# One image earlier through the steps: the norm, the statistics, a ScalarE copy and the ranking of a two-layer codebook convolution are moved

## The chip, the core and the metric

The kernel runs on one core of a Trainium2 chip. Its engines are TensorE (PE; its weight loads are listed as PEld), VectorE (DVE), ScalarE (ACT), GpSimd (POOL) and SyncE (SP, which here only issues DMAs). The metric is the device time of one execution in microseconds (us). Three runs of the kernel before gave 2716.25, 2726.48 and 2731.89 us; the median is 2726.48 us.

## What is computed

The input holds 16 images of 256 channels and 28 x 28 positions. Each image is normalised in groups of 8 channels (`_gn`), goes through two codebook convolutions with a batch norm each, through a squeeze-and-excitation gate, and is added to its input twice.

```python
def amm_conv3x3(x, centroids, w_sub, stride=1):
    p = patches(x, 3x3).reshape(B, C, 9, Ho * Wo).transpose(0, 3, 1, 2)
    d = sum(p * p) - 2.0 * einsum('bncs,cks->bnck', p, centroids) + sum(centroids * centroids)
    attn = softmax(-d)                                   # over 16 centroids of each channel
    lut = einsum('cks,cso->cko', centroids, w_sub)
    return einsum('bnck,cko->bno', attn, lut)
...
out = amm_conv3x3(x, centroids1, wsub1)
out = relu(bn_inference(out, ...))
out = amm_conv3x3(out, centroids2, wsub2)
out = se_layer(bn_inference(out, ...), se_w1, se_b1, se_w2, se_b2)
return relu(out + x)
...
x = x + _L0_conv_ref(_gn(x), ...)
```

## The kernel before, in words

All 16 images pass through layer 1, then all 16 through layer 2. An image of a layer is cut into four blocks: two halves of the channels (`hh`) times two halves of the rows (`t`). `BLOCKS` gives the order. Every block takes two steps, so an image takes eight; image n of the 32 (16 in each layer) starts at step g = 8n. "Step 0 to 7" below means the step within its image.

The order is written out by hand. `at(step, sub, function, ...)` puts a job into a table; the jobs are sorted by step and by `sub` and issued in that order. Every engine and every DMA queue takes its instructions strictly in the order of issue, so the place of a job decides behind what it waits.

Block j (g = 2j) goes this way:

- `patches` (L366, L370) loads the shifted rows of the image from its home in DRAM (`home1` in layer 1, `home2` in layer 2) into one of two patch buffers `pt`. It is issued two steps ahead, at `sub` 1.5, six DMAs on SyncE's queue for each half block.
- `logits` (L382) are 32 small matmuls on TensorE for a group of 32 channels (one of four: `mm`), two groups in each of two steps, at `sub` 0.1 and 1.1. `exps` (L393) on ScalarE follows each. In the first half of layer 2's channels, group 0 goes the `wide_` way through VectorE and GpSimd, so that the largest logit is subtracted.
- Two steps after its start, `num_b` (L446) makes the denominators and the last numerator; `split_r` (ScalarE), `join_r` and `recip_dve` (VectorE) turn them into reciprocals, and `spread` (L485, L489, VectorE shuffles) copies these to the rows of the numerators.
- Three steps after its start, `num_a` (L432) makes the other numerators in four rounds, in the order `SLOT_MM`. Each round writes its own pair of PSUM banks. A round is either multiplied by its spread reciprocal on VectorE (`scale_a`, L508) or copied on ScalarE (`copy_a`, L502) and multiplied on GpSimd (`scale_q`, L497). The rounds that ScalarE copies are called `kept`: before, the last round, and the last two where the next block is a wide one.
- `mix` (L523, L525, GpSimd) makes differences of numerators; `product` (L516, TensorE) multiplies numerators by the look-up tables, 63 k-slices an image in seven combinations. Seven steps of an image have nearly a full product; the product of step 7 has a single slice.

Because four pairs of PSUM banks rotate (`ROLES`), the second pair of the odd step's second logits takes the bank pair of numerator round 1, and the odd step's product that of round 2.

In layer 1 the next image is prepared beside this: `load_x` (L158) loads it to `xt`, `gn_stats` (L314, L315, VectorE), `gn_mean` and `gn_var` (TensorE, VectorE, and GpSimd at L254 to L341) make the statistics, `gn_apply` (L347, ScalarE) writes the normalised image into `xpads`, and `to_home1` (L359, SyncE) stores it twice to `home1`. The first patches of the next image are read from there; they are issued at step 6, `sub` 1.5. Layer 1's outputs are summed in `hpads`, normalised by `norm_out` (L567, ScalarE), and scattered by `to_home2` (L588, indirect DMAs on GpSimd's queue), one scatter waiting for the one before to land. In layer 2, `norm_both` (L580), `se_hidden`, `se_gate`, `se_recip` and the `finish_` jobs make the gate and the sums.

Image 0 of layer 1 gives the channels' ranking for layer 2: `rank_make`, `rank_sum`, `rank_look` and `rank_cols` make row numbers, and `h0_load` and `h0_put` put image 0's rows into `home2`.

Of the kernel before, what the change touches and what calls it, by code (L numbers as in the profile page):

```python
# [8 lines left out]
F32 = mybir.dt.float32  # L9
# [8 lines left out]
P = 128  # L18
# [20 lines left out]
KO = (2, 3, 4, 5, 6, 7, 8, 0, 1)  # L39
SLOT_MM = (1, 2, 3, 0)  # L40
BLOCKS = ((0, 0), (0, 1), (1, 1), (1, 0))
# [32 lines left out]
def kernel(  # L74
# [20 lines left out]
    nc = tc.nc  # L95
# [150 lines left out]
    nc.gpsimd.tensor_scalar(gmat, gmat, 1.0 / 8.0, None, op0=ALU.mult)  # L246
    mhalf = const.tile([P, NB], F32, name="mhalf")
    nc.gpsimd.memset(mhalf, -0.5)
    nc.vector.memset(xpads[0], 0.0)
# [560 lines left out]
    def se_gate(b, step=None):  # L810
        ps = small_bank("sep", step)[:, :NB]
        nc.tensor.matmul(ps, lhsT=w2_sb, rhs=se[b], start=True, stop=True)  # L812
        gt = small.tile([P, NB], F32, name="se_gt")
        for k in range(NB):
            nc.scalar.activation(  # L815
                gt[:, k : k + 1], ps[:, k : k + 1], AF.Exp, bias=nb2_sb[:, k : k + 1], scale=-1.0
            )
        se[b] = gt

    def se_recip(b):  # L820
        nc.vector.tensor_scalar_add(se[b], se[b], 1.0)  # L821
        nc.vector.reciprocal(se[b], se[b])  # L822
# [89 lines left out]
    for j, u in enumerate(blocks):  # L912
# [3 lines left out]
        for p in range(2):  # L916
            u["pt", p] = pts[p]
            at(g + p - NPT, 1.5, patches, u, p, nc.gpsimd if 0 < g + p < 5 else None)
            for q in range(2):
                mm = 2 * p + q  # L920
                at(g + p, 0.1 + q, logits, u, mm)
                if wide and mm == 0:
                    at(g, 0.12, wide_copy, u, mm)
                    at(g, 0.9, wide_turn, u, mm)
                    at(g, 1.38, wide_max, u, mm)
                    at(g, 1.39, wide_sub, u, mm)
                    at(g + 1, 1.22, wide_back, u, mm)
                    at(g + 1, 1.95, wide_exp, u, mm)
                else:
                    at(g + p, 0.12 + q, exps, u, mm)  # L930
        kept = SLOT_MM[2 if wide_next(j) else 3 :]
        at(g + 2, 1.0, num_b, u)
# [5 lines left out]
        for i, mm in enumerate(SLOT_MM):  # L938
# [3 lines left out]
            else:  # L942
                at(g + 2, 2.05 if i == 1 + (len(kept) == 1) else 1.4 + 0.01 * i, spread, u, mm)
                at(g + 3, 1.04 + 0.001 * i, scale_a, u, mm)
# [4 lines left out]
    for l in range(2):  # L949
        for b in range(B):  # L950
# [23 lines left out]
            if l == 0 or b == B - 1:  # L974
                at(g + 11, 1.9, norm_out, l, b, *c12)
                at(g + 11, 1.91, norm_out, l, b, *c22)
                at(g + 12, 1.9, norm_out, l, b, *c11)
                at(g + 13, 0.3, norm_out, l, b, *c21)
            else:
                for o in range(NB):  # L980
                    at(g + 12 + o, 0.3 if o else 1.9, norm_both, b, o)
            if l == 0:
# [8 lines left out]
                if b + 1 < B:  # L991
                    at(*((g - 2, 2.6) if b else (2, 1.65)), load_x, b + 1)
                    for q in range(NB):
                        at(*((g + q, 1.9) if b else (3, 1.9)), gn_stats, b + 1, q)
                    at(g + 3 - 2 * (b > 0), 2.1, gn_mean, b + 1, step=g + 3 - 2 * (b > 0))
                    at(g + 4 - (b > 0), 2.1, gn_var, b + 1, step=g + 4 - (b > 0))
                    for q in range(NB):
                        at(g + 5, 1.9, gn_apply, b + 1, q)
                        at(g + 5, 1.92, to_home1, b + 1, q)
            else:  # L1000
                last = b == B - 1
                at(*((g + 11, 0.6) if last else (g + 13, 2.6)), load_x, b, last)
                at(g + 13, 2.1, se_hidden, b, g + 13)
                at(*((g + 14, 1.05, se_gate, b, g + 14) if last else (g + 17, 2.1, se_gate, b, g + 17)))
# [28 lines left out]
    for o in range(2):  # L1033
        at(15, 1.9, rank_make, o)
        at(17, 1.9, rank_sum, o)
        at(17, 1.95, rank_look, o)
    for o in range(2):
        at(18 + o, 2.7, rank_cols, o)
        at(20 + 2 * o, 0.6, h0_load, o)
        for r in range(2):  # L1040
            at(*(((21, 1.77), (21, 1.808)), ((23, 2.7), (25, 1.78)))[o][r], h0_put, o, r)
        at(32 + 2 * o, 0.6, codes_load, o)
# [217 lines left out]
```

## Time and profile before

| What | Value |
|---|---|
| median of three runs | 2726.48 us |
| the profiled execution | 2734.72 us |
| its span in the profile | 2733.2 us |
| VectorE, ScalarE, GpSimd busy | 65%, 49%, 70% of the span |
| mean granted TensorE clock | 0.988 of full speed |
| data moved by DMA | 374.37 MB |

In the profile's rows the first figures are a start and a length in us, or, in a group, the sum of busy time and the mean of one instruction in ns. `L382` is line 382 of the kernel. `out<-in` names the tiles written and read. What stands in brackets is the engine's idle time in front of the instruction and what ended it: `[3.51 <-DMA pt<-home]` says that the engine stood 3.51 us until a DMA from `home` to `pt` had landed. `SPq` rows are DMAs that SyncE issues. A view of waits gives, for an instruction and what released it, the total in us, the number of times and the longest. The window view gives the busy time of each engine in a stretch, then the granted clock, the DMA engines' busy share and GB/s.

### The profile page before, as it was taken

What the parts mean: (1) busy time and instruction counts of PE and PEld (TensorE: products, weight loads), DVE (VectorE), ACT (ScalarE), POOL (GpSimd) and SP (SyncE); (2) the same over time, 40 slices, a digit from 0 to 9 for tenths busy, and PEclk for the clock granted to TensorE, in tenths of its full rate; (3) what the DMA queues carried; (4) which work ended last, traced back from release to release, by engine and by line L of the source; (5) the groups of instructions that cost most, each with busy time, mean ns of one, the idle gap of its engine ahead of it and who ended that gap; (6) DMA issues with size and microseconds to landing.
All of it is one profiled execution on the core that took longest, in us unless ns stands there. A gap on an engine that the chain in (4) does not pass through costs nothing. (4 is left out here: it accounts for less than half of the span.)

```text
span 2733.2 us, 85665 instructions
## 1 busy us (share of the span) xinstructions
PE 2636.8 (96%) x36984; PEld 1274.1 (47%) x36984; DVE 1785.9 (65%) x3802; ACT 1347.5 (49%) x1857; POOL 1902.5 (70%) x1333
## 2 busy tenths in 40 slices
PE   5899999999999999999999999999999999999997
PEld 2444444444444444444444444444444444444443
DVE  4666565566655566556567677677776786767675
ACT  2444444444444444444454555555555555555553
POOL 3755676656666567665577777877787877787786
PEclk9999999999999999999999999999999999999999
DMA  8665667755666666765485554545555545555541
GB/s 187 151 147 146 143 166 192 186 135 129 161 166 155 150 145 166 171 168 147 112 186 135 113 124 110 122 106 117 121 120 119 117 108 112 124 122 119 117 109 53
DMA packets 223335, 374.37 MB, mean 137 GB/s; under 512 B 30360, under 2 KB 193736, under 8 KB 222952
## 3 DMA queue, kind: packets, MB, share of 16 engines
q1 hardware_dynamic: 216008, 334.87, 54.0%
q0 software_dynamic: 6944, 33.95, 3.6%
q8 instruction: 295, 4.83, 0.8%
q14 instruction: 88, 0.72, 0.1%
HBM read 288.93 MB, written 79.80 MB: 135 GB/s over the span
## 5 line engine op out<-in xcount | busy, mean ns | idle before, releaser
L525 POOL TENSOR_TENSOR qp<-qp,qp 128x784 f32<-128x784 f32 x512 | 943.0, 1865 | 191.2 <-DVE qp L508 190.8
L393 ACT ACTIVATE e<-lg 128x784 f32<-128x784 f32 x960 | 739.2, 821 | 674.2 <-PE lg L382 667.2
L516 PE MATMUL acc<-qp,w_S 128*128 128x392 f32 x2048 | 739.5, 501 | 6.5 <-POOL qp L525 3.8
L382 PE MATMUL lg<-pt,wd 32*32 32x392 f32 x16384 | 516.0, 509 | 57.1 <-DMA pt<-home 49.7
L489 DVE STREAM_SHUFFLE rb<-r 128x392 f32<-128x392 f32 x1024 | 550.3, 603 | 0.0
L516 PE MATMUL acc<-qp,w_A 128*128 128x392 f32 x1536 | 546.5, 499 | 0.1
L516 PEld LDWEIGHTS acc<-qp,w_S 128*128 128x128 f32 x2048 | 375.8, 190 | 354.6 <-POOL qp L525 31.3
L460 DVE SCALAR_TENSOR_TENSOR r<-nb,kst,r 128x392 f32<-128x392 f32 x128 | 79.6, 622 | 568.3 <-ACT r L456 558.6
L516 PEld LDWEIGHTS acc<-qp,w_A 128*128 128x128 f32 x1536 | 284.1, 190 | 250.2 <-DVE qp L508 30.0
L446 PE MATMUL nb<-e,cwb 64*32 64x392 f32 x8192 | 389.7, 510 | 0.7 <-ACT e L393 0.7
L432 PE MATMUL na<-e,cwa 64*32 64x392 f32 x8192 | 376.1, 494 | 0.0
L508 DVE TENSOR_TENSOR qp<-na,rb 128x784 f32<-128x784 f32 x352 | 322.0, 967 | 38.0 <-PE na L432 29.4
L474 DVE RECIPROCAL r<-r 128x392 f32<-128x392 f32 x128 | 333.2, 2603 | 4.4
L497 POOL TENSOR_TENSOR qp<-qp,rb 128x784 f32<-128x784 f32 x160 | 296.8, 1865 | 3.2 <-ACT e L393 0.4
L382 PEld LDWEIGHTS lg<-pt,wd 32*32 32x32 f32 x16384 | 131.9, 103 | 347.4 <-issue 235.1
L497 POOL TENSOR_TENSOR qo<-qo,rb 128x392 f32<-128x392 f32 x128 | 131.3, 1026 | 215.2 <-DVE rb L485 215.1
L446 PEld LDWEIGHTS nb<-e,cwb 64*32 64x32 f32 x8192 | 187.4, 110 | 199.7 <-issue 49.2
L432 PEld LDWEIGHTS na<-e,cwa 64*32 64x32 f32 x8192 | 185.1, 106 | 181.9 <-issue 83.9
L502 ACT COPY qp<-na 128x784 f32<-128x784 f32 x160 | 126.9, 814 | 137.7 <-PE na L432 134.6
L456 ACT ACTIVATE r<-nb,kst 128x392 f32<-128x392 f32 x128 | 86.7, 678 | 185.3 <-PE nb L446 183.2
L588 POOL DMA_INDIRECT home<-hpad,col x60 | 60.4, 1007 | 159.2 <-DMA home<-hpad,col 85.8
L417 POOL TENSOR_TENSOR z<-z,mx 128x1568 f32<-128x1568 f32 x32 | 92.0, 2876 | 97.8 <-DVE mx L411 97.8
(153 smaller groups left out, 1768.2 us busy)
## 6 DMA issues: line engine op xcount, KB each, us to landing
pt<-home SPq DMA_DIRECT2D x768, 209.0 KB
pt<-home SPq DMA_DIRECT2D x756, 104.5 KB
home<-xpad SPq DMA_DIRECT2D x31, 899.0 KB
xt<-in_x SPq DMA_DIRECT2D x30, 784.0 KB
out_dram<-y SPq DMA_DIRECT2D x32, 392.0 KB
w_S<-d_wS SPq DMA_DIRECT2D x4, 576.0 KB
st<-in_wsub SPq DMA_DIRECT2D x4, 512.0 KB
st<-d_wa SPq DMA_DIRECT2D x16, 128.0 KB
```

Of the source, the lines that this page charges most:

```text
L382: nc.tensor.matmul(bk[32 * c : 32 * c + 32, :N].rearrange("p (r w) -> p r w", w=W), lhsT=wts["wd", u["hh"]][32 * i : 32 * i + 32, mm, c, : ...
L393: nc.scalar.activation(eg[:, 2 * i : 2 * i + 2, :], bk[:, :, :N], AF.Exp, scale=2.0)
L417: nc.gpsimd.tensor_tensor(zk, zk, mx.unsqueeze(2).to_broadcast([P, N // 4, K]), ALU.subtract)
L432: nc.tensor.matmul(bs[32 * i : 32 * i + 32, r, :N], lhsT=wts["cwa", u["hh"]][64 * r : 64 * r + 64, mm, i, :], rhs=es[64 * r : 64 * r + 64, ...
L446: nc.tensor.matmul(bs[32 * i : 32 * i + 32, r, :N], lhsT=wts["cwb", u["hh"]][64 * r : 64 * r + 64, mm, i, :], rhs=es[64 * r : 64 * r + 64, ...
L474: nc.vector.reciprocal(u["r"], u["r"])
L489: nc.vector.stream_shuffle(rb[:, r, :], u["r"], mask_of(2 * mm + r))
L497: nc.gpsimd.tensor_tensor(q, q, u.pop(("rb", mm)), ALU.mult)
L502: nc.scalar.copy(pair(u, mm), u.pop(("na", mm))[:, :, :N])
L508: nc.vector.tensor_mul(pair(u, mm), u.pop(("na", mm))[:, :, :N], rb)
L516: nc.tensor.matmul(accs[key][:, :N], lhsT=wl[w][:, k, :], rhs=us["q", k], start=first and n == 0, stop=last and n == len(ks) - 1,)
L525: nc.gpsimd.tensor_tensor(pair(out_u, mm), pair(in0, mm), pair(in1, mm), ALU.subtract)
```

## The change

All of it is a matter of where jobs stand in the order, but for one instruction that changes its engine. Step numbers are those within the image.

- From the second image on, `gn_apply` and `to_home1` of the next image go from step 5 to step 4, with the same `sub`. For the first image they stay in step 5.
- `gn_stats` of the next image's two halves, one at the end of step 0 and one at the end of step 1, both go to the head of step 0 (`sub` 0.3).
- `SLOT_MM` is (1, 0, 2, 3) and `kept` picks round 1, or rounds 1 and 3 in front of a wide block. So ScalarE copies the second round of numerators, where it copied the last, and VectorE scales the others. Group 0 is the one copied, as before.
- On ScalarE, layer 1's last `norm_out` goes from `sub` 0.3 to 1.06 of step 5, behind `copy_a`; layer 2's second `norm_both` from 0.3 to 1.9 of step 5; `wide_exp` from 1.95 to 1.89.
- The gate's addition of 1 goes from VectorE (in `se_recip`) to ScalarE (in `se_gate`), as an Identity with a bias tile `one`; `se_hidden` goes a step later except for the last image.
- `rank_make` for the second half of the channels goes one step later, the sums and look-ups from step 17 to 18, the columns one step later, and image 0's loads and puts are spread anew.

```diff
-SLOT_MM = (1, 2, 3, 0)
+SLOT_MM = (1, 0, 2, 3)
...
+    one = const.tile([P, 1], F32, name="one")
+    nc.gpsimd.memset(one, 1.0)
...
+        nc.scalar.activation(gt, gt, AF.Identity, bias=one, scale=1.0)
         se[b] = gt
     def se_recip(b):
-        nc.vector.tensor_scalar_add(se[b], se[b], 1.0)
         nc.vector.reciprocal(se[b], se[b])
...
-                    at(g + 1, 1.95, wide_exp, u, mm)
+                    at(g + 1, 1.89, wide_exp, u, mm)
...
-        kept = SLOT_MM[2 if wide_next(j) else 3 :]
+        kept = SLOT_MM[1 : 4 if wide_next(j) else 2 : 2]
...
-                at(g + 2, 2.05 if i == 1 + (len(kept) == 1) else 1.4 + 0.01 * i, spread, u, mm)
+                at(g + 2, 2.05 if i == 4 - len(kept) else 1.4 + 0.01 * i, spread, u, mm)
...
-                at(g + 13, 0.3, norm_out, l, b, *c21)
+                at(g + 13, 1.06, norm_out, l, b, *c21)
...
-                    at(g + 12 + o, 0.3 if o else 1.9, norm_both, b, o)
+                    at(g + 12 + o, 1.9, norm_both, b, o)
...
-                        at(*((g + q, 1.9) if b else (3, 1.9)), gn_stats, b + 1, q)
+                        at(*((g, 0.3) if b else (3, 1.9)), gn_stats, b + 1, q)
...
-                        at(g + 5, 1.9, gn_apply, b + 1, q)
-                        at(g + 5, 1.92, to_home1, b + 1, q)
+                        at(g + 5 - (b > 0), 1.9, gn_apply, b + 1, q)
+                        at(g + 5 - (b > 0), 1.92, to_home1, b + 1, q)
...
-                at(g + 13, 2.1, se_hidden, b, g + 13)
+                at(g + 14 - last, 2.1, se_hidden, b, g + 14 - last)
...
-        at(15, 1.9, rank_make, o)
-        at(17, 1.9, rank_sum, o)
-        at(17, 1.95, rank_look, o)
+        at(15 + o, 1.9 + 0.2 * o, rank_make, o)
+        at(18, 2.1, rank_sum, o)
+        at(18, 2.15, rank_look, o)
...
-        at(18 + o, 2.7, rank_cols, o)
-        at(20 + 2 * o, 0.6, h0_load, o)
+        at(19 + o, 2.7, rank_cols, o)
+        at(20 + 3 * o, 0.6, h0_load, o)
...
-            at(*(((21, 1.77), (21, 1.808)), ((23, 2.7), (25, 1.78)))[o][r], h0_put, o, r)
+            at(*(((21, 1.77), (22, 2.95)), ((24, 2.95), (25, 1.78)))[o][r], h0_put, o, r)
```

In these lines `g` is the first step of the image, so `g + 13` is step 5 of the image after it, where an image's last outputs come out, and `b` is the image whose step it is.

## The prediction

> **What bounds the kernel now.** I read the page first, then the image cadence in TensorE's timeline, then its waits and its instruction groups in two long windows, and last one change of image in detail.
>
> ```profile
> span 2733.2 us, 85665 instructions
> ...
> PE 2636.8 (96%) x36984; PEld 1274.1 (47%) x36984; DVE 1785.9 (65%) x3802; ACT 1347.5 (49%) x1857; POOL 1902.5 (70%) x1333
> ```
>
> TensorE is busy 96% of the span, so only its gaps and its slow stretches can be won. The first `nb` matmuls of an image's first step come at fixed places of the order, so their starts measure an image (start us, length us, engine, line, operation, names):
>
> ```profile
> 105.37 5.05 PE L446 MATMUL nb<-e,cwb 64*32 64x392 f32 x64
> ...
> 1304.19 2.90 PE L446 MATMUL nb<-e,cwb 64*32 64x392 f32 x64
> ...
> 1385.99 2.89 PE L446 MATMUL nb<-e,cwb 64*32 64x392 f32 x64
> ...
> 2600.93 2.89 PE L446 MATMUL nb<-e,cwb 64*32 64x392 f32 x64
> ```
>
> The first two rows are 14 images of layer 1 apart: (1304.19 - 105.37) / 14 = 85.63 us. The last two are 15 images of layer 2 apart: 81.00 us. Both layers give TensorE the same products, so layer 1 loses 4.6 us an image, 14 x 4.63 = 65 us in all. TensorE's waits in the window 110 to 1320 us (total, times, longest) name 38 us of that:
>
> ```profile
> PE lg L382 <- DMA pt<-home: 33.7, 12, 5.3
> PE lg L382 <- DVE half_sum L553: 2.3, 1, 2.3
> PE acc L516 <- POOL qp L525: 1.7, 4, 0.8
> ```
>
> Another 20 us are inside the busy time. Two groups in that window and then, for layer 2, in 1420 to 2630 us (busy us, mean ns, idle before):
>
> ```profile
> L382 PE MATMUL lg<-pt,wd 32*32 32x392 f32 x7264 | 230.3, 511 | 36.8 <-DMA pt<-home 33.7 <-DVE half_sum L553 2.3 <-ACT e L393 0.3
> L446 PE MATMUL nb<-e,cwb 64*32 64x392 f32 x3600 | 176.0, 520 | 0.0
> ```
> ```profile
> L382 PE MATMUL lg<-pt,wd 32*32 32x392 f32 x7648 | 234.1, 499 | 0.5 <-issue 0.5
> L446 PE MATMUL nb<-e,cwb 64*32 64x392 f32 x3840 | 174.8, 492 | 0.0
> ```
>
> Per `nb` matmul that is 48.9 ns of busy time against 45.5 ns, 12.1 us over 3600; per `lg` matmul 31.7 against 30.6 ns, 8.0 us over 7264. A wait in TensorE's timeline and the stretch of one us at its end (PE, PEld, DVE, ACT, POOL busy, granted clock, DMA share, GB/s) tell why:
>
> ```profile
> 1134.36 1.62 PE L382 MATMUL lg<-pt,wd 32*32 32x392 f32 x32 [2.48 <-DMA pt<-home]
> ```
> ```profile
> 1134.00:1135.00 1.00, 0.64 (x17) 0.32 (x32) 0.00 (x0) 0.00 (x0) 1.00 (x2) 0.50 1.03 171
> ```
>
> The granted clock is 0.50: behind a wait the logits and the `nb` matmuls run at half speed, and they are the groups that follow every change of image.
>
> Here is one such change (image 5 to 6): the last `lg` of step 6, the short product of step 7, and the first logits of the next image, with SyncE's issues.
>
> ```profile
> 523.83 0.94 PE L382 MATMUL lg<-pt,wd 32*32 32x392 f32 x32
> ...
> 534.82 0.93 PE L516 MATMUL acc<-qp,w_S 128*128 128x392 f32 x2
> 539.26 1.12 PE L382 MATMUL lg<-pt,wd 32*32 32x392 f32 x32 [3.51 <-DMA pt<-home]
> 540.31 4.33 PE L446 MATMUL nb<-e,cwb 64*32 64x392 f32 x64
> ```
> ```profile
> 518.82 1.75 SPq L359 DMA_DIRECT2D home<-xpad  x2
> ...
> 528.61 0.59 SPq L366 DMA_DIRECT2D pt<-home  x1
> ...
> 532.74 0.39 SPq L158 DMA_DIRECT2D xt<-in_x  x1
> ```
> ```profile
> SPq L366 <- DMA home<-xpad: 88.7, 16, 8.2
> ```
>
> The patch buffer is free at 524.8, but the patches leave only at 528.61: the last row (SyncE's waits over the whole run) says that 16 times, 5.5 us each on average, they waited for the store of the normalised image. They would have to land by 535.75 and land 3.5 us later. The order of steps makes it so: the store stands in step 5, its reader in step 6.
>
> **The change part by part.**
>
> *Norm and store in step 4.* The store gains a whole step, 10 to 11 us, against a longest wait of 8.2 us, so the patches can leave when their buffer is free. In the example they leave 3.5 us sooner (0.3 us after 524.8), and from first issue to logits took 539.26 - 528.61 = 10.65 us against 535.75 - 525.1 = 10.65 us available: the edge. I leave 0.2 us at each of 14 changes of image, 33.7 - 3 = **-30.7 us**. Image 0 to 1 keeps its old place and its wait, outside the window. The half clock goes with the waits: 12.1 + 8.0 = 20.1, of which I give 2 to VectorE's lateness (below): **-18 us**.
>
> The Trainium skill's page "TensorE: Matmul & The Clock Gate" (section "What's actually happening") says that the array falls to half its clock after an idle window of about 3.4 us and recovers after as long a busy one. No run here shows a fixed threshold: the wait in front of the 0.50 above was 2.48 us. By the page alone the shorter waits (33.7 / 12 = 2.8 us on average) would have cost no clock, half of the 18 us would not be there to win, and the time would be some 9 us higher.
>
> What pays for it in step 4: two norms on ScalarE and the store on SyncE. ScalarE's and GpSimd's rows around that place, an image later:
>
> ```profile
> 676.64 0.72 ACT L567 ACTIVATE hpad<-hpad,bnsh,bnsc 128x392 f32<-128x392 f32 x1
> 681.58 0.83 ACT L393 ACTIVATE e<-lg 128x784 f32<-128x784 f32 x1 [4.22 <-PE lg L382]
> ...
> 687.30 1.98 ACT L347 ACTIVATE xpad<-xt,nrm 128x784 f32<-128x784 f32 x2
> ```
> ```profile
> 673.08 0.25 POOL L341 TENSOR_SCALAR nrm<-nrm 128x2 f32<-128x2 f32 x1
> ...
> 686.81 1.02 POOL L497 TENSOR_TENSOR qo<-qo,rb 128x392 f32<-128x392 f32 x1 [4.06 <-DVE rb L485]
> ```
>
> The two norms take 1.98 us and fall into ScalarE's 4.22 us of idle time; their scale is ready at 673.3, they would start at 677.4. Cost nothing; without that cover 2 us in front of the exps. The store's 1.2 to 1.8 us of issue stand behind step 4's patches and in front of step 5's, which wait for their buffer longer than that.
>
> *Statistics at the head of step 0.* Two pairs leave the places behind the spreads of steps 0 and 1, where VectorE is late for the numerators. Its row from that place, and TensorE's:
>
> ```profile
> 545.62 0.62 DVE L460 SCALAR_TENSOR_TENSOR r<-nb,kst,r 128x392 f32<-128x392 f32 x1 [8.89 <-ACT r L456]
> ...
> 555.50 1.21 PE L382 MATMUL lg<-pt,wd 32*32 32x392 f32 x32
> 556.79 4.19 PE L516 MATMUL acc<-qp,w_S 128*128 128x392 f32 x12
> ```
>
> From `lg` to product 1.29 us pass instead of 0.94: 0.35 us an image, 4.9 us over 14. The new place is the 8.89 us in front of `join_r`; behind a change of image without a wait some 4 us of them remain, and the pairs take 2 x (1.04 + 0.21) = 2.5 us.
>
> *Second numerator round by ScalarE, the other norms later, se's +1 on ScalarE.* The product takes the bank of round 2, which VectorE's second multiplication now frees instead of its third (about 0.9 us sooner), while ScalarE frees that of round 1 beside it. In layer 2 the addition to the gate is what makes VectorE late (min / median / max ns), and TensorE shows it in the same image:
>
> ```profile
> L821 DVE TENSOR_SCALAR se_gt<-se_gt x16: 170/2688/2758, 1568.0 to 2723.5; 128x2 f32<-128x2 f32 x16
> ```
> ```profile
> 1905.82 1.43 PE L382 MATMUL lg<-pt,wd 32*32 32x392 f32 x32
> 1907.17 4.22 PE L516 MATMUL acc<-qp,w_A 128*128 128x392 f32 x12
> ```
>
> An addition of two elements that takes 0.17 us alone holds VectorE 2.69 us, and the product comes 1.35 us behind `lg`: 0.41 us an image, 6 us over 15. ScalarE gets a short ACTIVATE in its place, an estimate of 0.3 us by its other small ones, off the path but at the very end. Together with the 4.9 us above 10.9; not every image need show it, and ScalarE's copy may itself come late now and then, so I take **-9 us** (bounds: +13 if the copy holds the second pair of `lg` banks by 0.2 us in half of the 128 odd steps, -11 if all goes).
>
> *Ranking.* VectorE waited for GpSimd between the two halves of `rank_make`, and a put of image 0's rows blocked GpSimd in front of the mixes; both places move away: 2.3 + 1.7 us of the waits above, **-4 us**.
>
> *Moved with no price.* The last norm of layer 1's step 5 goes behind ScalarE's copy (0.72 us, row 676.64) and stays in front of the scatter that reads it; layer 2's second norm, `se_hidden` and the wide exp change places within ScalarE's idle time, and what they feed comes a step later at the earliest. The table rows' puts of image 0 and the rank lookups go past mixes and loads in GpSimd's and SyncE's queues, but in image 2 and 3 only: at worst a wait like the 1.7 us above stands elsewhere.
>
> *What is added.* 1.5 us for longer landings (bounds in the rivals). Sum: -30.7 - 18 - 9 - 4 + 1.5 = -60.2 us. The profiled execution took 2734.72 us around its span of 2733.2 (1.5 us outside it), 8.2 us above the median of 2726.48. What varies should be mostly the waits that go, so I don't shift the result: 2734.7 - 60.2 = **2674.5 us**. Crosscheck: with layer 1 at layer 2's 81.0 us and 6 us won in layer 2 it is 2734.7 - 64.8 - 6 = 2664.
>
> **The rivals.**
>
> *The image arrives late for its statistics* (slower). Its load stands behind the patches, 4.1 us after their first issue, so at about 529.2 in the example; without the wait, `join_r` stands 4.9 us behind the end of the short product (the 6.36 us of 539.26 to 545.62 less the 4.33 - 2.89 = 1.44 us by which its `nb` was slow), at 540.7. The statistics must start by 538.2, 9 us after the load's issue; about 1.5 us more are free, since one pair left the later place and the product needs one multiplication less. The two landings the trace shows, in the first two images beside weight loads:
>
> ```profile
> 48.76 0.59 SPq L158 DMA_DIRECT2D xt<-in_x  x1
> ...
> 95.79 0.50 SPq L158 DMA_DIRECT2D xt<-in_x  x1
> ...
> 111.49 0.55 SPq L366 DMA_DIRECT2D pt<-home  x1
> ```
> ```profile
> 58.64 1.04 DVE L314 BATCH_NORM_STATS2 gn_st<-xt 128x6 f32<-128x392 f32 x2 [0.93 <-DMA xt<-in_x]
> ```
>
> One took 58.64 - 48.76 = 9.9 us, the other up to 15.7 us (SyncE's wait that ended at 111.49 was for this load). At 9.9 nothing is lost. At 15.7 VectorE is 5.2 us late, `join_r`, the reciprocal, the spreads and the multiplications queue behind it, and TensorE waits as long: 14 x 5.2 = 73 us and 18 us of half clock, 2674.5 + 91 = **2766 us**. It eats the whole gain from about 14.5 us on. Later loads have no weights beside them, hence 5 in 100.
>
> *The store beside the scatters.* In step 4 GpSimd scatters half of `home2` and waits for it to land before the second scatter; now the store runs beside it. The only scatter with the store beside it:
>
> ```profile
> 258.82 1.01 POOL L588 DMA_INDIRECT home<-st,col  x1 [0.15 <-issue]
> ...
> 264.82 0.96 POOL L588 DMA_INDIRECT home<-st,col  x1 [3.73 <-DMA home<-st,col]
> ```
>
> Six us from issue to the next. If the store makes that 12, GpSimd's 4.06 us of idle time (686.81) cover all but 2 us, and the mixes hold the product: 14 x 2 = 28 us, **2702 us**. The page "DMA: Bandwidth & Descriptors" of the Trainium skill (section "Issuing engines are not separate DMA queues") lets transfers of all queues interleave on the same 16 engines; by it the scatter must slow down, though it gives no size. 9 in 100.
>
> *The patches stay late by themselves.* Scatter and image load share their time. If half of the 3.5 us gained is lost again, 1.8 x 14 = 25 us and some clock remain: **2704 us**. 8 in 100.
>
> *The store is no sooner* because ScalarE or the statistics hold it: then only the 13 us of ranking and VectorE are won, 2722 us. 6 in 100.
>
> **How the numbers follow.** The forecast, 2654 to 2690, has 70 in 100 (low end: the crosscheck less 10 us, should layer 1's images, which lack the gate and the finish, fall below 81); 2 in 100 lie below it. The second and third rivals end between 2690 and 2712. A measurement here can tell about 0.5% from no change: faster is below 2712.8, slower above 2740.1. So faster 0.70 + 0.02 + 0.09 + 0.08 = 0.89, same 0.06, slower 0.05. The range 2654 to 2706 leaves out the slow rival, the unchanged one and the ends.
>
> **What would show it.** Right: TensorE's wait for patches in layer 1 falls below 10 us, SyncE's for the store to a few; `nb` takes 45 to 46 ns each in both layers; layer 1's images take 81 to 82 us; the gate's 2.7 us are gone. Wrong: a VectorE wait of L314 for the image, GpSimd waits of some 12 us at L588, or ScalarE's L502 in front of `lg`.

## The result and the profile after

| | before | after |
|---|---|---|
| median of 4 runs each, us | 2725.23 (2716.25 to 2731.89) | 2681.32 (2679.53 to 2684.49) |
| profiled execution, us | 2734.72 | 2684.49 |
| its mean granted clock | 0.988 | 0.993 |

The four runs of before are the three named above and a fourth. The ratio after to before is 0.9842, 95% interval 0.9812 to 0.9873: the kernel is 1.6% faster. The forecast was 2674.5 us and the range 2654 to 2706. From profiled run to profiled run the change gave 50.2 us where 60.2 were forecast; from median to median it gave 43.9 us. In the kernel after, the lines quoted here stand two lines lower (logits L384, `nb` L448, `na` L434, products L518, scatters L590, statistics L316, patches L368).

The page of the kernel after opens so:

```profile
span 2683.0 us, 85705 instructions
...
PE 2613.8 (97%) x36984; PEld 1261.1 (47%) x36984; DVE 1773.8 (66%) x3786; ACT 1354.7 (50%) x1873; POOL 1903.7 (71%) x1334
```

TensorE's busy time fell by 23.0 us and the span by 50.2, so 27.2 us were idle time. Nearly all of it is in layer 1, as one row of the windows view for each kernel shows. Its columns are the window and its length, then the busy time of PE, PEld, DVE, ACT and POOL, the granted clock, the DMA share and GB/s. Each window runs from 110 us to the first `nb` of layer 1's last image, so both hold the same 14 images but for some 0.5 us. First before, then after:

```profile
110.00:1304.19 1194.19, 1153.32 (x16115) 559.03 (x16099) 728.90 (x1713) 531.64 (x726) 767.87 (x610) 0.98 0.64 156
```
```profile
110.00:1264.31 1154.31, 1140.58 (x16067) 552.21 (x16066) 739.05 (x1706) 529.97 (x725) 768.19 (x609) 1.00 0.64 161
```

Layer 1 won 1194.19 - 1154.31 = 39.9 us. TensorE's idle time went from 1194.19 - 1153.32 = 40.9 to 1154.31 - 1140.58 = 13.7 us (-27.1), its busy time fell by 12.7 us, and the granted clock rose from 0.98 to 1.00. (The lists of waits leave out idle pieces below 0.15 us, so their sums are a little smaller.) TensorE's waits of the kernel after in the window 110 to 1320 us (total, times, longest; the full list has eleven groups, 13.6 us):

```profile
PE acc L518 <- POOL qp L527: 3.7, 6, 1.5
PE lg L384 <- DVE qp L510: 2.2, 1, 2.2
...
PE lg L384 <- ACT hpad L549: 1.0, 1, 1.0
...
PE lg L384 <- DMA pt<-home: 0.8, 1, 0.8
```

The wait for patches fell from 33.7 us (12 times) to 0.8 us (once). The other waits are new or have grown: 13.6 - 0.8 = 12.8 us against 5.7 before, waits for GpSimd's mixes, VectorE's multiplications and ScalarE's copy first. The change of image that the prediction took apart (5 to 6) now looks like this, in SyncE's and TensorE's timelines:

```profile
512.10 0.55 SPq L368 DMA_DIRECT2D pt<-home  x1
...
515.82 0.39 SPq L158 DMA_DIRECT2D xt<-in_x  x1
```
```profile
523.42 0.93 PE L518 MATMUL acc<-qp,w_S 128*128 128x392 f32 x2
524.27 1.04 PE L384 MATMUL lg<-pt,wd 32*32 32x392 f32 x32
525.24 2.86 PE L448 MATMUL nb<-e,cwb 64*32 64x392 f32 x64
```

The patches leave at 512.10 and the logits follow the short product without a wait; `nb` takes 2.86 us where it took 4.33.

The groups that the half clock had slowed, in layer 1 (window 110 to 1320 us), and `nb` again in layer 2 (1420 to 2630):

```profile
L384 PE MATMUL lg<-pt,wd 32*32 32x392 f32 x7456 | 228.6, 500 | 7.4 <-DVE qp L510 2.2 <-issue 1.5 <-DVE rb L491 1.1
L448 PE MATMUL nb<-e,cwb 64*32 64x392 f32 x3712 | 174.7, 492 | 1.3 <-issue 1.0 <-DVE gn_dv L328 0.3
```
```profile
L448 PE MATMUL nb<-e,cwb 64*32 64x392 f32 x3840 | 174.4, 492 | 0.0
```

In layer 1 `nb` went from 48.9 to 174.7 / 3712 = 47.1 ns and `lg` from 31.7 to 30.7 ns: 6.6 and 7.6 us at the earlier counts, 14.2 us together. Layer 2's `nb` takes 45.4 ns, so some 6 us of difference are left in layer 1.

By the starts of the `nb` groups, an image of layer 1 took 82.81 us (before: 85.63) and one of layer 2 80.49 (81.00). That is 39.4 us over 14 images, 7.6 over 15, and some 3 us elsewhere. Below, a "step" is the time from the first `nb` or `na` matmul of one step to that of the next, averaged over images 3 to 14 in layer 1 and over the images of layer 2.

### The profile page after: what moved, and what is told of

Its sections match the earlier page's. It is cut to its first block, busy times and chain, and to the rows that moved or that the text cites. A ratio compares the mean times of both kernels' runs of the same rounds, so it can differ in the third digit from the quotient of the medians.

```text
span 2683.0 us, 85705 instructions
## 1 busy us (share of the span) xinstructions
PE 2613.8 (97%) x36984; PEld 1261.1 (47%) x36984; DVE 1773.8 (66%) x3786; ACT 1354.7 (50%) x1873; POOL 1903.7 (71%) x1334
## 4 chain that ended last, share of the span: by engine, by line
PE 86%; DMA 1%; POOL 1%; issue 1%; DVE 1%; ACT 0%; SPq 0%; POOLq 0%; DVEq 0%; ACTq 0%
PE acc L518 46%; PE lg L384 15%; PE na L434 12%; PE nb L448 12%; DMA home<-hpad,col 1%; POOL qp L527 1%; PE sep L814 0%; ACT e L395 0%; DMA pt<-home 0%; PE sep L803 0%; DVE qp L510 0%; DVE rb L491 0%; POOL home L590 0%; POOL qo L525 0%; PE sqp L288 0%
## 5 line engine op out<-in xcount | busy, mean ns | idle before, releaser
L518 PE MATMUL acc<-qp,w_S 128*128 128x392 f32 x2048 | 743.2, 503 | 7.7 <-POOL qp L527 6.3
L518 PE MATMUL acc<-qp,w_A 128*128 128x392 f32 x1536 | 546.5, 499 | 0.1
L518 PEld LDWEIGHTS acc<-qp,w_S 128*128 128x128 f32 x2048 | 376.1, 190 | 356.6 <-POOL qp L527 39.1
L384 PE MATMUL lg<-pt,wd 32*32 32x392 f32 x16384 | 500.6, 504 | 27.0 <-DMA pt<-home 16.3
L518 PEld LDWEIGHTS acc<-qp,w_A 128*128 128x128 f32 x1536 | 284.1, 190 | 247.9 <-DVE qp L510 37.6
L510 DVE TENSOR_TENSOR qp<-na,rb 128x784 f32<-128x784 f32 x352 | 334.1, 972 | 98.1 <-PE na L434 84.9
L448 PE MATMUL nb<-e,cwb 64*32 64x392 f32 x8192 | 382.4, 497 | 2.1 <-issue 1.0
L434 PE MATMUL na<-e,cwa 64*32 64x392 f32 x8192 | 377.5, 494 | 0.1
L448 PEld LDWEIGHTS nb<-e,cwb 64*32 64x32 f32 x8192 | 181.4, 107 | 195.8 <-issue 57.1
L384 PEld LDWEIGHTS lg<-pt,wd 32*32 32x32 f32 x16384 | 127.5, 103 | 309.0 <-issue 261.6
L434 PEld LDWEIGHTS na<-e,cwa 64*32 64x32 f32 x8192 | 182.5, 106 | 186.8 <-issue 78.0
L590 POOL DMA_INDIRECT home<-hpad,col x60 | 60.6, 1011 | 185.9 <-DMA home<-hpad,col 91.2
L504 ACT COPY qp<-na 128x784 f32<-128x784 f32 x160 | 130.1, 813 | 26.0 <-PE na L434 24.0
```

The costliest lines, as they stand in the source:

```text
L384: nc.tensor.matmul(bk[32 * c : 32 * c + 32, :N].rearrange("p (r w) -> p r w", w=W), lhsT=wts["wd", u["hh"]][32 * i : 32 * i + 32, mm, c, : ...
L434: nc.tensor.matmul(bs[32 * i : 32 * i + 32, r, :N], lhsT=wts["cwa", u["hh"]][64 * r : 64 * r + 64, mm, i, :], rhs=es[64 * r : 64 * r + 64, ...
L448: nc.tensor.matmul(bs[32 * i : 32 * i + 32, r, :N], lhsT=wts["cwb", u["hh"]][64 * r : 64 * r + 64, mm, i, :], rhs=es[64 * r : 64 * r + 64, ...
L504: nc.scalar.copy(pair(u, mm), u.pop(("na", mm))[:, :, :N])
L510: nc.vector.tensor_mul(pair(u, mm), u.pop(("na", mm))[:, :, :N], rb)
L518: nc.tensor.matmul(accs[key][:, :N], lhsT=wl[w][:, k, :], rhs=us["q", k], start=first and n == 0, stop=last and n == len(ks) - 1,)
```

## The experiments

My theory was that the store's place is what the change is worth: 47 of the 60 us, with VectorE's lateness and the ranking for the rest. The rivals were that the norm is worth less and the small moves more, and that the store beside the scatters takes part of it back. Twelve kernels follow. Each has its own median of 4 runs (5 for the last of the store runs), with the kernel before on the same chip beside it; before gave medians of 2718 to 2725 us there.

| run | median us (lowest to highest) | ratio to before, 95% |
|---|---|---|
| norm_alone | 2697.15 (2694.39 to 2700.54) | 0.9911 (0.9891 to 0.9931) |
| norm_undone | 2700.01 (2695.25 to 2703.13) | 0.9920 (0.9899 to 0.9942) |
| rank_undone | 2684.95 (2680.28 to 2688.99) | 0.9871 (0.9852 to 0.9890) |
| stats_undone | 2682.54 (2680.27 to 2683.39) | 0.9846 (0.9818 to 0.9875) |
| round_undone | 2687.71 (2686.72 to 2698.24) | 0.9875 (0.9839 to 0.9910) |
| add_undone | 2678.81 (2678.07 to 2683.19) | 0.9836 (0.9806 to 0.9865) |
| round_add_undone | 2690.56 (2684.45 to 2693.92) | 0.9898 (0.9868 to 0.9927) |
| wide_exp_undone | 2684.35 (2680.49 to 2685.66) | 0.9851 (0.9825 to 0.9877) |
| norms_undone | 2685.25 (2683.99 to 2689.20) | 0.9855 (0.9830 to 0.9880) |
| store_in_step_3 | 2681.70 (2680.66 to 2684.62) | 0.9857 (0.9839 to 0.9875) |
| store_3_var_sooner | 2668.47 (2668.03 to 2677.03) | 0.9803 (0.9771 to 0.9836) |
| store_3_var_rank_18 | 2669.48 (2665.91 to 2672.82) | 0.9799 (0.9776 to 0.9821) |

**The norm and the store alone** (kernel before, with one edit), **and everything but them** (kernel after, with the same edit undone).

```diff
-                        at(g + 5, 1.9, gn_apply, b + 1, q)
-                        at(g + 5, 1.92, to_home1, b + 1, q)
+                        at(g + 5 - (b > 0), 1.9, gn_apply, b + 1, q)
+                        at(g + 5 - (b > 0), 1.92, to_home1, b + 1, q)
```

> The kernel before with one part of the change alone: the norm and the store of the next image in step 4. Theory A (the forecast): the patch waits and the half clock behind them go, 30.7 + 18 us less 1.5, so about 2678 us against 2725, and TensorE's wait for patches in the window 110 to 1320 us falls from 33.7 to some 3 us. Theory B (the store now runs beside the scatters and delays GpSimd and ScalarE by 0.5 to 1 us an image): the waits go as well, but only 35 to 40 us are won, 2685 to 2690 us, and the stretch from the first scatter of an image's second pair to the pair before it grows from about 5.5 to 7.5 us.

> The changed kernel with the norm and the store of the next image back in step 5. Theory A: the rest of the change wins 13 us by itself, about 2712 us. Theory B: the rest wins as much as the changed kernel does less what the norm alone wins, so with a norm worth 35 to 40 us it comes to 2716 to 2721 us. In both, the patch waits are back at 30 us or more in layer 1, and layer 2's images stay at 80.5 us.

Measured: 2697.15 and 2700.01 us. The norm alone wins 25.6 us against its own runs of before (2722.74), the rest alone 22.7; added they give 48.3, together they gave 43.9. From profiled run to profiled run the norm alone gave more, 2734.72 - 2697.68 = 37.0 us, since the profiled execution of before (2734.72) was slower than all four runs of its median. In the run with the norm alone TensorE never waits for patches in layer 1; the wait that leads its list, in image 2, and the list's head of the run without the norm:

```profile
PE lg L382 <- DVE half_sum L553: 7.5, 1, 7.5
PE acc L516 <- POOL qp L525: 4.2, 2, 4.0
```
```profile
PE lg L384 <- DMA pt<-home: 23.9, 8, 5.5
PE lg L384 <- DVE half_sum L555: 4.9, 3, 1.7
```

The mechanism stands: with the early store the patches' wait is gone, and without it 23.9 of the 33.7 us are there (the expectation was 30 or more). But both time forecasts missed, in opposite directions: the norm is worth less than the 47 us I gave it, the rest more than the 13.

**What the rest is made of.** Six kernels, each the kernel after with one part put back.

*Ranking* (`rank_make` to `h0_put` at their old places):

```diff
-        at(15 + o, 1.9 + 0.2 * o, rank_make, o)
-        at(18, 2.1, rank_sum, o)
-        at(18, 2.15, rank_look, o)
+        at(15, 1.9, rank_make, o)
+        at(17, 1.9, rank_sum, o)
+        at(17, 1.95, rank_look, o)
...
-        at(19 + o, 2.7, rank_cols, o)
-        at(20 + 3 * o, 0.6, h0_load, o)
+        at(18 + o, 2.7, rank_cols, o)
+        at(20 + 2 * o, 0.6, h0_load, o)
...
-            at(*(((21, 1.77), (22, 2.95)), ((24, 2.95), (25, 1.78)))[o][r], h0_put, o, r)
+            at(*(((21, 1.77), (21, 1.808)), ((23, 2.7), (25, 1.78)))[o][r], h0_put, o, r)
```

> The changed kernel with the ranking jobs at their old places. Theory A (the forecast's term of 4 us is won by moving them): 2685 us, image 2 of layer 1 longer than 92.3 us. Theory B (the second half of rank_make now stands in front of VectorE's multiplications in step 17 and costs what the move wins): 2679 to 2682 us, image 2 at 90 to 92.5 us, and TensorE's 2.25 us wait for VectorE's multiplication in step 17 is gone.

Measured: 2684.95 us, 3.6 more, though the runs overlap. The 7.5 us wait for `half_sum` is back; image 2 takes 95.2 us instead of 92.3. Put back in the changed kernel, the old places cost some 3 us. Against the kernel before, the waits of image 2 hardly fell: the 2.3 us in step 0 went, but the mixes of step 6, which took 1.7 us there, still take 1.5, and the move left a stall of its own, in VectorE's and TensorE's timelines of the kernel after:

```profile
198.71 0.98 DVE L650 TENSOR_SCALAR row<-row,score 128x256 f32<-128x256 f32 x1
199.61 1.93 DVE L651 TENSOR_SCALAR row<-row,score 128x256 f32<-128x256 f32 x1
201.47 2.72 DVE L510 TENSOR_TENSOR qp<-na,rb 128x784 f32<-128x784 f32 x3
```
```profile
202.48 1.36 PE L384 MATMUL lg<-pt,wd 32*32 32x392 f32 x32 [2.25 <-DVE qp L510]
203.77 5.46 PE L518 MATMUL acc<-qp,w_S 128*128 128x392 f32 x12
```
```profile
203.00:204.00 1.00, 1.00 (x31) 0.23 (x2) 1.00 (x2) 0.17 (x1) 1.00 (x1) 0.50 0.06 16
```

The second half of `rank_make`, moved to the end of step 16, stands in front of VectorE's multiplications (L510) in step 17. The logits wait 2.25 us for a bank, and behind that wait the granted clock (third number from the end) is 0.50 and the product takes 5.46 us instead of 4.22. The whole step takes 14.81 us; before it was 10.96.

*Statistics* (each half back at the end of its step):

```diff
-                        at(*((g, 0.3) if b else (3, 1.9)), gn_stats, b + 1, q)
+                        at(*((g + q, 1.9) if b else (3, 1.9)), gn_stats, b + 1, q)
```

> The changed kernel, but with the two halves of the next image's statistics back at the ends of steps 0 and 1 of an image (norm and store stay in step 4). Theory A, that the place of the statistics made VectorE late at the products of those steps: step 1 goes back from 10.83 towards 11.23 us in layer 1, 0.4 us at each of 14 images, about 2685 to 2688 us against 2681. Theory B, that what the earlier place gave is spent by the seven waits of VectorE for the image in the changed kernel (13.1 us on VectorE, though TensorE shows few of them): within 2 us of the changed kernel, 2679 to 2683 us, with the group 'gn_st <- DMA xt' gone from the waits.

Measured: 2682.54 us, theory B. Step 1 of layer 1 stays at 10.84 us (10.83 in the kernel after, 11.23 before), so it was not their place that made it long. VectorE's waits for the image are there in the kernel after (first fence, window 110 to 1320 us) and all but gone here (second, whole run), and neither shows in the time:

```profile
DVE gn_st L316 <- DMA xt<-in_x: 8.3, 5, 3.0
```
```profile
DVE gn_st L316 <- DMA xt<-in_x: 0.2, 1, 0.2
```

*Round order, the gate's addition, and both*:

```diff
-SLOT_MM = (1, 0, 2, 3)
+SLOT_MM = (1, 2, 3, 0)
...
-        kept = SLOT_MM[1 : 4 if wide_next(j) else 2 : 2]
+        kept = SLOT_MM[2 if wide_next(j) else 3 :]
...
-                at(g + 2, 2.05 if i == 4 - len(kept) else 1.4 + 0.01 * i, spread, u, mm)
+                at(g + 2, 2.05 if i == 1 + (len(kept) == 1) else 1.4 + 0.01 * i, spread, u, mm)
```
```diff
-        nc.scalar.activation(gt, gt, AF.Identity, bias=one, scale=1.0)
         se[b] = gt

     def se_recip(b):
+        nc.vector.tensor_scalar_add(se[b], se[b], 1.0)
```

> The changed kernel, but with the rounds of the numerators in the old order, so that ScalarE copies the old round and VectorE multiplies the others. Theory A, that the round that ScalarE copies carries most of what the change gives beside the norm (22.7 us in the run with norm and store put back, where I had counted 13): 2691 to 2697 us, with TensorE's wait for VectorE's products back in both layers and the copies of ScalarE waiting for 'na' some 126 times, as in the kernel before. Theory B, that the round is worth little: 2680 to 2684 us.

> The changed kernel, but with the +1 of the gate back on VectorE, as four numbers added behind ScalarE's exponentials. Theory A, that VectorE's wait for those exponentials held up the work behind it once an image of layer 2 (step 3 of the second layer's images is 0.38 us shorter in the changed kernel): 2685 to 2688 us, with that step back at 11.1 us. Theory B, that this 0.38 us is another part's doing (the round): within 2 us, 2679 to 2683 us, with the step left at 10.7 us and VectorE's wait hidden.

> The changed kernel, but with both the old order of the numerators' rounds and the gate's +1 back on VectorE. Each of these alone left step 3 of layer 2 at 10.72 and 10.73 us, though the addition still held VectorE 2.76 us. Theory A, that in the kernel before the two together made VectorE late in that step, so that undoing either one is covered by the other: step 3 back at 11.07 us as in the run with the norm alone, some 5 us over 15 images, about 2692 to 2694 us against 2687.7 with the round order alone undone. Theory B, that the addition was never on the path: step 3 at 10.7 us and 2686 to 2689 us.

Measured: the round 2687.71 us, 6.4 more and between the theories, most of it in layer 1 (83.19 us an image for 82.81, step 1 at 11.04 us for 10.83); the addition 2678.81, theory B; both 2690.56, on a chip where before ran at 2718.21. Step 3 of layer 2 tells them apart: 11.09 us before, 10.71 after, 10.72 with the round put back, 10.73 with the addition put back, **11.13 with both**. TensorE's rows of that step in one image, with the addition alone back and then with both:

```profile
1938.30 0.94 PE L384 MATMUL lg<-pt,wd 32*32 32x392 f32 x32
1939.17 4.22 PE L518 MATMUL acc<-qp,w_A 128*128 128x392 f32 x12
```
```profile
1942.36 1.42 PE L384 MATMUL lg<-pt,wd 32*32 32x392 f32 x32
1943.71 4.22 PE L518 MATMUL acc<-qp,w_A 128*128 128x392 f32 x12
```

From `lg` to product it is 0.87 us with the addition alone and 1.35 with both, as in the kernel before. So the 2.7 us that the addition holds VectorE did lengthen this step, as predicted, but only with the old round order behind it: the new order covers it, and so does the addition's move without the new order. Each edit alone brings what both bring; 0.4 us in 15 images is paid for twice.

*Wide exponential, and the norms of step 5*:

```diff
-                    at(g + 1, 1.89, wide_exp, u, mm)
+                    at(g + 1, 1.95, wide_exp, u, mm)
```
```diff
-                at(g + 13, 1.06, norm_out, l, b, *c21)
+                at(g + 13, 0.3, norm_out, l, b, *c21)
...
-                    at(g + 12 + o, 1.9, norm_both, b, o)
+                    at(g + 12 + o, 0.3 if o else 1.9, norm_both, b, o)
```

> The changed kernel, but with the wide exponential of layer 2's first two blocks back behind ScalarE's two finish norms at the end of a step (1.95 in place of 1.89). Layer 2's step 3 is 0.38 us shorter in the changed kernel, and it stayed short with the gate's addition back on VectorE and with the old round order. Theory A, that the place of the wide exponential is what shortened it: step 3 of layer 2 back at 11.1 us in 15 images, 5.7 us, about 2685 to 2688 us. Theory B, that several edits each cover it: step 3 stays at 10.7 us and the time within 2 us of the changed kernel's 2681.

> The changed kernel, but with the norm of step 5 in both layers (one norm_out in layer 1, the second norm_both in layer 2) back at the head of that step, in front of ScalarE's copies. Layer 2's step 5 is 0.29 us shorter in the changed kernel and layer 1's 0.08 us. Theory A, that the place of the norm did that: step 5 of layer 2 back at 11.0 us in 15 images, 4.4 us, and some in layer 1, about 2685 to 2688 us. Theory B, that ScalarE's idle time covers it, as I had costed it: within 2 us, 2679 to 2683 us.

Measured: 2684.35 us, 3.0 more and between the theories, and 2685.25 us, 3.9 more and as theory A. Behind ScalarE's finish norms the wide exponential is 0.2 us late once an image, in front of `nb` (layer 2, window 1420 to 2630 us), and step 3 takes 10.95 us:

```profile
PE nb L448 <- ACT e L427: 2.8, 14, 0.2
```

With the norms at the head of step 5, ScalarE's and TensorE's rows of one image:

```profile
1882.43 1.04 ACT L582 ACTIVATE y<-y,bnsh,bnsc 128x784 f32<-128x784 f32 x1
...
1883.45 0.81 ACT L504 COPY qp<-na 128x784 f32<-128x784 f32 x1
```
```profile
1883.73 1.47 PE L384 MATMUL lg<-pt,wd 32*32 32x392 f32 x32
1885.13 4.22 PE L518 MATMUL acc<-qp,w_A 128*128 128x392 f32 x12
```

The norm (L582) stands in front of ScalarE's copy of the second round (L504), which ends at 1884.26; the second half of `lg` needs that round's bank, and the product comes 1.40 us behind the start of `lg` instead of 0.87. Step 5 of layer 2 takes 11.22 us against 10.71. No idle time is listed: the wait hides in the length of the `lg` group.

That is not what step 5 cost in the kernel before, though. Its step 5 took 11.01 us with the norm at the head, and 0.21 of the 0.30 us that it lost are four small matmuls of the gate (L803), which went to step 6 with `se_hidden`: step 6 of layer 2 grew from 10.06 to 10.27 us. The norm's late place is needed because, with the new round order, the copy behind it frees a bank that `lg` waits for. The move of `se_hidden` had no run of its own.

Put back one by one, these parts cost 3.6 (ranking), 1.2 (statistics), 6.4 (round), -2.5 (addition), 3.0 (wide exponential) and 3.9 us (norms): 15.6 together. From the norm alone to the full change it is 2697.15 - 2681.32 = 15.8 us. That the two agree is partly chance: each difference is uncertain by several us (the runs of one kernel spread by 3 to 12 us, on different chips), and parts that cover each other don't add up. With the 9.2 us of the pair in place of 6.4 - 2.5 the sum is 20.9.

**The store beside the scatters.** Three kernels take the store away from step 4, where it runs beside GpSimd's scatters of `home2`.

```diff
-                    at(g + 4 - (b > 0), 2.1, gn_var, b + 1, step=g + 4 - (b > 0))
+                    at(g + 4 - 2 * (b > 0), 2.1, gn_var, b + 1, step=g + 4 - 2 * (b > 0))
                     for q in range(NB):
-                        at(g + 5 - (b > 0), 1.9, gn_apply, b + 1, q)
-                        at(g + 5 - (b > 0), 1.92, to_home1, b + 1, q)
+                        at(g + 5 - 2 * (b > 0), 1.9, gn_apply, b + 1, q)
+                        at(g + 5 - 2 * (b > 0), 1.92, to_home1, b + 1, q)
```

> The changed kernel with the variance in step 2 and the norm and the store in step 3, one step further ahead, in front of the scatters and no longer beside them. Theory A (once the patches needn't wait, the place of the store does not matter): 2680 to 2682 us as the changed kernel. Theory B (the store beside the scatters costs 0.6 us in step 6 of an image and more in images 2 and 5): 2668 to 2674 us, step 6 of layer 1 back from 10.96 to about 10.4 us or less, and ScalarE's waits of 6.7 and 9.0 us for a scatter in front of the first copy of step 6 gone.

Measured: 2681.70 us, no change. The prediction's rival did happen in the kernel after, at a smaller size. Who waits for the scatters, before, after, and with the store in step 3 (window 110 to 1320 us in each):

```profile
POOL home L588 <- DMA home<-hpad,col: 72.0, 15, 6.8
```
```profile
POOL home L590 <- DMA home<-hpad,col: 77.8, 19, 7.3
ACT hpad L549 <- DMA home<-hpad,col: 15.7, 2, 9.0
```
```profile
POOL home L590 <- DMA home<-hpad,col: 73.8, 13, 6.7
PE na L434 <- DVE gn_var L338: 11.1, 14, 1.0
ACT hpad L549 <- DMA home<-hpad,col: 4.7, 1, 4.7
```

With the store beside them the scatters are waited for longer, and ScalarE's first copy of step 6, which overwrites what a scatter reads, waits for one twice. One edit apart, the run without the early norm has 65.7 us of GpSimd's waits and none of ScalarE's. In all 14 traces the two together are 82 to 104 us where the store stands in step 4 (nine kernels) and 66 to 79 us where it stands elsewhere (five). Step 6 of layer 1 went from 10.14 to 10.67 us with the change and back to 10.28 with the store in step 3 (10.11 with the norm undone). That is a mean of unequal images: image 5 alone took 13.17 us, and image 2, which the mean leaves out, 15.45 against 13.48 before. But the last fence has a new wait, 14 times 0.8 us, in front of the numerators, and step 2 went from 10.83 to 11.69. `gn_var`, now in an even step, gets the PSUM bank that the next step's first round of numerators uses, and VectorE reads it only behind its last spreads. So I set it ahead of them:

```diff
-                    at(g + 4 - 2 * (b > 0), 2.1, gn_var, b + 1, step=g + 4 - 2 * (b > 0))
+                    at(g + 4 - 2 * (b > 0), 2.03 if b else 2.1, gn_var, b + 1, step=g + 4 - 2 * (b > 0))
```

> The run with the store in step 3, but with the variance matmul and VectorE's read of it set ahead of VectorE's last spreads of that step, so that the PSUM bank is read before the first round of numerators needs it. Theory A, that the 11.1 us of waits of 'na' for 'gn_var' (14 of 0.8 us) were all that ate the gain of a store away from the scatters: about 2671 us, with that group gone from TensorE's waits and step 2 of layer 1 back from 11.69 towards 10.9 us. Theory B, that the gain isn't there, or that the spreads behind the read come late in its place (VectorE's products then wait for 'rb'): 2677 to 2682 us.

Measured: **2668.47 us**, theory A. Step 2 is back at 11.02 us, step 6 at 10.17, an image of layer 1 takes 81.91 us, and image 2 87.6 instead of 92.3. The same waits here:

```profile
POOL home L590 <- DMA home<-hpad,col: 72.7, 13, 7.2
ACT hpad L549 <- DMA home<-hpad,col: 4.7, 1, 4.7
PE na L434 <- DVE gn_var L338: 1.6, 1, 1.6
```

Last, the ranking's second half out of step 17 as well:

```diff
-        at(15 + o, 1.9 + 0.2 * o, rank_make, o)
+        at(15 + 3 * o, 0.4 if o else 1.9, rank_make, o)
```

> The run with the store in step 3 and the variance read sooner, and with the second half of the ranking moved from the end of step 16 to early in step 18. Theory A, that its two long VectorE instructions in front of the multiplications of step 17 are what keeps image 2 at 87.6 us: the wait of 'lg' for VectorE's products there (2.2 us) and the half clock behind it go, image 2 falls to 83 to 84 us, about 2664 to 2665 us against 2668.5. Theory B, that the ranking holds VectorE as much in step 18: within 2 us of 2668.5.

Measured: 2669.48 us, no gain. The wait in step 17 is gone, and image 2 takes 86.1 instead of 87.6 us, but TensorE now waits two steps later:

```profile
221.63 0.95 PE L384 MATMUL lg<-pt,wd 32*32 32x392 f32 x32 [1.42 <-DVE qp L510]
```

## Why the prediction was right, and where it was off

The mechanism was right, and the time lies in the range, 6.8 us above the forecast. That it came so near is partly luck: the store's place was sized too large (47 us forecast, 25.6 measured alone) and the rest too small (13 forecast, 22.7 measured alone), so that two errors partly cancelled. Step by step, in the profiled runs (rounded):

| | forecast us | measured us |
|---|---|---|
| waits of layer 1: patches | -30.7 | -32.9 |
| waits of layer 1: all others | -4 (ranking), +1.5 | +5.8 |
| TensorE's busy time in layer 1 | -18 (clock), -3 to -5 (VectorE) | -12.7 |
| layer 2 (image 16 lost 1.7 us, in step 6) | -4 to -6 | -7.6 |
| elsewhere | 0 | -2.7 |
| sum | -60.2 | -50.2 |

- *Patches.* Right: 33.7 to 0.8 us, SyncE's waits for the store in front of its first patch DMA 88.7 us (16) to 10.7 us (4), with 2.9 us more at the second (L372).

```profile
SPq L368 <- DMA home<-xpad: 10.7, 4, 5.3
```

- *Half clock*, -18. Too large: `nb` and `lg` gave 14.2 us. I had put all of the difference between the two layers down to the clock behind the waits. Some 6 us of difference were in `nb` when the waits had gone. Of the 15 `nb` groups behind a change of image, those longer than 3.0 us fell from 9 to 4; of the 15 in step 6 they rose from 1 to 9. One of these, and a stretch of 1 us inside it with the granted clock:

```profile
920.06 3.81 PE L448 MATMUL nb<-e,cwb 64*32 64x392 f32 x64
```
```profile
921.00:922.00 1.00, 1.00 (x25) 0.81 (x31) 0.00 (x0) 0.89 (x2) 1.00 (x1) 1.00 0.82 276
```

  This `nb` takes 0.9 us more than the usual 2.92 at full clock, so something else stretches it. With the store in step 3 the long ones in step 6 are 2 to 4 of 15, and with the store in step 4 they are 6 to 11 in eight kernels, but 2 in the ninth (round order and addition both undone). So the store's neighbourhood is likely, and not shown. The Trainium skill's page "TensorE: Matmul & The Clock Gate" (section "What's actually happening") names an idle window of about 3.4 us for the lower clock, and by it only 9 of the 18 us were there to win; 14.2 us came back, and the 0.50 behind the 2.25 us wait of step 17 is a second case below that length.

- *Added waits*, forecast +1.5 for landings. Undersized, and the largest error of the sum in TensorE's idle time: the other waits of layer 1 rose from 5.7 to 12.8 us, where they were to fall by 4. Of these, 2.2 us are the ranking's second half in step 17, a term that I had put at nothing, and 4.7 us the mixes and a copy in step 6 of images 2, 5 and 9, behind the scatters (1.7 us of such waits were there before). The other 5.8 us are nine short waits in other places, 1.2 us of them as before; no run explains them. The rival "the store beside the scatters" was priced at 28 us; step 6 grew by 0.53 us, some 7 us over 14 images. With the store in step 3 and the variance read early, 12.8 us came back by the medians (some 11 by the ratios to before).
- *VectorE's lateness*, -9, the size about right and its causes half wrong. Step 1 of layer 1 lost 0.40 us, where 0.35 were forecast, but not by the statistics: put back, they cost 1.2 us, within the spread of the runs, and left that step as it was. With the old round order half of it returns (11.04 us). The addition's 0.4 us an image in layer 2 was read rightly, but it needed the old round order. The wide exponential and the norms, at no price in the prediction, cost 3 to 4 us each when put back behind the new round order. They lie on ScalarE, whose mean idle time I had taken for cover. What the prediction feared from ScalarE's copy, that it holds the second `lg` banks, is just what happens with the norm back in front of it.
- *Image late for the statistics.* VectorE does wait: 4.4 us for image 1 and up to 3.0 us later (seven times, 13.1 us), against the 5.2 of the rival. The run with the statistics back, where 0.2 us of it are left, is no faster, so TensorE hardly feels it. The reason I gave against this rival was wrong: loads of table weights (`st<-in_wsub`) do stand beside later images, in the kernel before at 412.8 to 524.5 us.
- *Not shifting the result from the profiled run.* The runs of after lie within 5.0 us and those of before within 15.6, but that what varied went with the waits is not shown: the runs of the kernel with the old round order, whose store is early, spread by 11.5 us. And the profiled run stood above the median of before, and counting from it made the gain 60 where from the median it was 52.
- *What would show it.* Held: patches below 10 us, the gate's 2.7 us gone, no scatter wait of 12 us, no ScalarE copy of numerators (L504) in front of `lg`. Missed: `nb` at 45 to 46 ns (47.1 in layer 1) and images of 81 to 82 us (82.81; image 2 alone, at 92.3 us, adds 0.7 to the mean). One sign of being wrong did show, VectorE's waits for the image.

## What to carry to other kernels

Where a transfer becomes early by a move, look first at what it now runs beside and which buffers and banks change hands there: here that took back 11 to 13 us, and a PSUM bank read 0.8 us late hid the better place from a first trial. Undo parts singly and in pairs: two edits that each cover the same loss show nothing when one of them is undone. That an engine is idle half of the time is no cover for a moved instruction; what decides is whether it then stands in front of the one copy or exponential that frees a bank.

## What the runs showed of the hardware

An addition of two elements a partition on VectorE took 2.75 us beside GpSimd's instructions. One image of the run with the addition back, VectorE's and GpSimd's rows:

```profile
1922.68 3.68 POOL L499 TENSOR_TENSOR qp<-qp,rb 128x784 f32<-128x784 f32 x2
1924.62 2.75 DVE L823 TENSOR_SCALAR se_gt<-se_gt 128x2 f32<-128x2 f32 x1
1926.31 2.14 POOL L562 TENSOR_TENSOR y<-y,half_sum 128x392 f32<-128x392 f32 x2
```
```profile
L823 DVE TENSOR_SCALAR se_gt<-se_gt x16: 170/2758/2855, 1522.4 to 2667.6; 128x2 f32<-128x2 f32 x16
```

It starts inside GpSimd's second multiplication (which ends at 1926.36) and ends at 1927.37, halfway through GpSimd's two additions (1926.31 to 1928.45). The Trainium skill's page "SBUF — State Buffer" (section "SBUF: two separate sides") has an exclusive lock on a port pair that GpSimd's instructions and some of VectorE's share, held for a whole instruction while the other side waits. The row fits it, with 2.75 us in place of the 0.17 us that the shortest of the 16 took, the last one, at 2667.6, beside an idle GpSimd (last fence: min, median and max in ns). That it waited past the end of one GpSimd instruction and through the next, no run explains.

A store did slow the scatters beside it. Where the two kernels differ in the store's place alone, GpSimd's waits for scatters in layer 1 rose from 65.7 to 77.8 us in the one pair and from 72.0 to 88.6 us in the other (kernel before and norm alone), and ScalarE's from nothing to 15.7 and 14.4 us. The page "DMA: Bandwidth & Descriptors" (section "Issuing engines are not separate DMA queues") of the Trainium skill says that DMAs of all issuing engines run on the same 16 DMA engines and interleave, which fits; it gives no size.
